# Zero rows of the later experts written inside the experts' loop of a one-core mixture-of-experts kernel

## The chip, the cores and the metric

The kernel runs on one core of a Trainium2 chip. The metric is the device time of one execution in microseconds (us); of several runs the median is taken. A core has five engines that work side by side, each through its own instructions in their order: TensorE (PE, matmuls and transposes), VectorE (DVE), ScalarE (ACT), GpSimd (POOL) and SyncE (SP). In this kernel SP does nothing but issue transfers (DMAs); ACT issues a few, and POOL issues all those whose rows are chosen by an index. Engines wait for each other and for transfers through semaphores.

## The reference, cut to what matters

The input `x` is 8,192 tokens of 256 numbers. It is normalised; one branch runs a gated recurrence over it, the other a mixture of 32 experts, of which each token takes four, plus a shared expert. The two are multiplied and added to `x`.

```python
xn = _layernorm(x)
s = recurrence(xn, W_in, b_in, W_g, b_g, W_out, b_out)
# ffn(xn):
w, idx = _gate(xf, wg)                      # 4 of 32 experts a token
cap = int(1.25 * N * K / E)                 # 1280 slots an expert
pos = (jnp.cumsum(oh, axis=0) * oh).sum(-1) - 1
dest = jnp.where(pos < cap, fe * cap + pos, E * cap)
xe = xp[buf_tok].reshape(E, cap, DIM)       # slots without a token are zero
h = silu(xe @ w1) * (xe @ w3)
out = (h @ w2) * buf_w
y = zeros.at[buf_tok].add(out)              # back to the tokens
z = (silu(xf @ sw1) * (xf @ sw3)) @ sw2     # shared expert
return x + s * silu(y + z)
```

So an expert has up to 1,280 slots, filled from the front with the tokens that chose it. How many are filled is known only when all tokens have been routed.

## The kernel before, in words

**First stage.** The tokens come in nine batches (`RTS`, 512, 512, then 1,024 each). For each batch the kernel normalises, turns rows into columns on PE, computes gates and logits, chooses experts on DVE (`choose`), finds each token's slot (`place`), and scatters the token's row into a DRAM buffer `xd_d` by POOL (`dispatch`, `send`, L517 to L527): one indirect DMA for 128 tokens and one of their four choices. A row is `XR` = 289 floats (1,156 bytes): the 256 features, 32 weights, and the token's number. The batches of the last round are sent by column of choice, the fourth first, since the slots are sorted downward: rows of expert 0 can stand only in the fourth column, rows of expert 1 in the third or fourth, and so on. Beside that the shared expert is computed for 16 chunks of 512 tokens; its output `zt` of a chunk is stored to `y_d` by a DMA (`shared_out`, L573 to L582) that SP issues, for the last two chunks ACT.

**Zero rows.** `xd_d` gives each expert 1,280 rows and 128 more. When all batches are routed, `ends()` (L535) computes on DVE, for each expert, the row behind its last token (`last[0, 1, e]`), and for each tile of 128 slots where to read it (`start`). `fill(e0, e1)` (L529 to L533) then has SP write, for each expert from `e0` to `e1`, 128 rows of zeros (`hole`) from that row on: a value load of the row number into a register, then a DMA of 144.5 KB. It is called four times, each time for a quarter of the experts: the first quarter right behind `ends()`, the second behind the output of shared chunk 12, both in the batch loop's turn r = 8 (L717 and L724), the third and the fourth in the turn r = 9 (L696 and L724), which has no batch of its own, only the rest of the shared expert and of the recurrence. In this turn SP first loads expert 0's weights (L690).

**Experts' loop.** `load_slots(e, i)` (L746 to L760) has SP read expert e's slots: part i of `spans`, 512, 512 and 256 slots, so 4, 4 and 2 DMAs of 128 rows, each behind a value load (L753, L754). Tiles `xe` of parts 0 and 1 share four buffers, those of part 2 two. Tile's tracking of `xd_d` makes each read wait for what wrote to it; the calls of `declare_no_dep` and `add_manual_dep` there replace that, for the first experts, by waits for the columns that can hold their rows. `load_expert(e)` (L117) loads 3 x 256 KB of weights into one of two buffers. Ahead of the loop SP has: the three parts of expert 0, the weights of expert 1, the three parts of expert 1 (L954 to L958).

A turn of the loop (L964) for expert e: SP issues parts 0 and 1 of expert e + 2; `hidden(e)` computes both projections, in sums and differences of quarter blocks so that seven products do the work of eight; PE then turns expert e + 1's slots (`turn`, L795); `first_out(e)` and `rest(e)` do the second projection and POOL adds the weighted rows to `y_d` at their tokens (L871); SP loads the weights and part 2 of expert e + 2.

All engines except POOL run in the order in which the code is written (`manual_schedule`). Within the first expert this order is, on DVE: `weight_sums(0)`, the blocks `B` of `second_blocks` (L809 to L812), `targets(0)` (`rf`, L769, which reads the last column of all three parts), then the sums `u`, `v` of `hidden(0)` (L826). On ACT: the copies into `B` (L803, L804, L808), `weights(0)` (`wt`, L776, which reads all three parts), then `p` (L841) and the copies of `v` (L846). On PE: `turn(0, 0)`, `turn(0, 1)`, four first products (`put`, L820), three added ones (`add_to`, L823), the same again for the second projection:

```python
            put(0, w(0, 0), B[:, 0])
            nc.scalar.copy(p, ps[0])
            put(1, S[:, 1, i], B[:, 4])
            plus(u, p, ps[1])
```

**Semaphores of transfers.** The transfers that SP and ACT issue take eight completion semaphores in turn, in the order of the program. An issue waits until the transfer before it on the same semaphore has landed.

**Tail.** 16 chunks of `y_d` are read back, passed through silu, multiplied by the recurrence's output and added to `x`.

Of the kernel before, what the change touches and what calls it, by code (L numbers as in the profile page):

```python
# [8 lines left out]
F32 = mybir.dt.float32  # L9
# [7 lines left out]
def recurrent_moe_kernel(  # L17
# [18 lines left out]
    nc = tc.nc  # L36
    P = 128
# [3 lines left out]
    E = wg.shape[0]  # L41
    H = w1.shape[2]
    K = 4
# [13 lines left out]
    XR = D + E + 1  # L57
# [4 lines left out]
    NR = len(RTS)  # L62
# [5 lines left out]
    FIRST = P  # L68
    END = FIRST + E * EP
# [10 lines left out]
    keep = ctx.enter_context(tc.tile_pool(name="keep", bufs=1))  # L80
# [8 lines left out]
    xd_d = dram.tile([END + P, XR], F32, name="xd_d")  # L89
# [6 lines left out]
    last = keep.tile([1, 2, E], I32, name="last")  # L96
# [7 lines left out]
    def apart(key, ins):  # L104

        tc.declare_no_dep(ins.ins, group=key, reason="different rows")
        tc.add_to_no_dep_group(key, ins.ins)
# [9 lines left out]
    def load_expert(e):  # L117
        w = wpool.tile([P, 3, KD, H], F32, tag="w", name=f"w_{e}")
        for i, src in enumerate((w1, w3, w2)):
            nc.sync.dma_start(out=w[:, i], in_=src[e].rearrange("(k p) h -> p k h", p=P))  # L120
        return w
# [20 lines left out]

    ET = mybir.EngineType
    engines = {ET.PE, ET.DVE, ET.Activation, ET.SP}
    with tc.tile_pool(name="ab", bufs=1) as ab, tc.tile_pool(name="xp", bufs=4) as xp, tc.tile_pool(
        name="rt", bufs=2
    ) as rt, tc.tile_pool(name="sh", bufs=2) as sh, tc.manual_schedule(engines=engines):
# [2 lines left out]
        def load_x(r):  # L150
            xt = xp.tile([P, RT, XR], F32, tag="xt", name=f"xt_{r}")
            for h in range(0, RTS[r], CT):
                nc.sync.dma_start(out=xt[:, h : h + CT, 0:D], in_=batch(x_f, r)[:, h : h + CT, :])
            xts[r] = xt
# [15 lines left out]
        for i, src in enumerate((sw1, sw3, sw2)):  # L170
# [8 lines left out]
            out=tri, in_=tri, compare_op=ALU.is_gt, fill=0.0, base=0, pattern=[[1, P]], channel_multiplier=-1  # L179
# [4 lines left out]
        for r0, n in ((0, 2), (2, NR - 2)):  # L184
            q = RTS[r0]
# [19 lines left out]
        hole = ab.tile([P, XR], F32, name="hole")  # L205
# [27 lines left out]
        with nc.allow_non_contiguous_dma(reason="a bias, once"):  # L233
# [13 lines left out]
            out=y_d[N : N + CAP, :].rearrange("(i p) d -> p i d", p=P),  # L247
            in_=hole[:, 0:D].unsqueeze(1).to_broadcast([P, EJ, D]),
# [278 lines left out]
                tc.add_to_no_dep_group(f"column{column}", ins.ins)  # L527

        def fill(e0, e1):  # L529

            for e in range(e0, e1):
                row0 = nc.sync.value_load(last[0:1, 1, e : e + 1], min_val=FIRST, max_val=END - P)  # L532
                apart("xd", nc.sync.dma_start(out=xd_d[bass.ds(row0, P), :], in_=hole))  # L533

        def ends():  # L535

# [147 lines left out]
        for r in range(4, NR + 1):  # L684
            new = r < NR
            c = 2 * (r - 2)
            if r + 2 < NR:
                load_x(r + 2)
            if r == NR:
                first_w = load_expert(0)  # L690
            if new:
                to_features(r, 0)
            project(r - 1, 0)
            shared_out(c - 1, late)
            if r == NR:
                fill(2 * E // 4, 3 * E // 4)  # L696
            if new:
                l0 = features(r, 0)
                to_features(r, 1)
            project(r - 1, 2)  # L700
            if new:
                l1 = features(r, 1)
                lg = ps_tp.tile([P, RT, E], F32, tag="tp", name=f"lg_{r}")
                logits(lg, l0, 0)
                logits(lg, l1, 1)
                M, cum, ex = choose(r, lg)
                weigh(r, M, ex)
            hT = shared_hidden(c)
            project(r - 1, 4)
            project(r - 1, 6)  # L710
            if new:
                pc = count(r, cum)
                put = place(r, M, cum, pc)
                dispatch(r, put)
                if r + 1 == NR:
                    ends()
                    fill(0, E // 4)  # L717
                recur(unit[r])
            if r + 1 < NR:
                norm(r + 1)  # L720
            shared_out(c, hT)
            if r + 1 >= NR:
                q = 2 * (r + 1 - NR) + 1
                fill(q * E // 4, (q + 1) * E // 4)  # L724
            late = shared_hidden(c + 1)
            if new:
                order_states(r)
            if r + 2 < NR:
                scale(r + 2)
# [8 lines left out]
    with tc.tile_pool(name="fin", bufs=NX, reuse_waits="tile") as fin, tc.manual_schedule(  # L738
        engines=engines
    ), ExitStack() as stack:  # L740
        mp = stack.enter_context(tc.tile_pool(name="moe", bufs=2, reuse_waits="tile"))
        ws, xes, rows, wts, Ss, Bs, hTs = {0: first_w}, {}, {}, {}, {}, {}, {}

        rows_of = mybir.DependencyInfo(mybir.DependencyClass.Sync, mybir.DependencyReason.DATA)

        def load_slots(e, i):  # L746
            s0, n = spans[i]
            xe = xes[e, i] = mp.tile(
                [P, n // P, XR], F32, tag=f"xe{n}", bufs=4 if n == CW else 2, name=f"xe_{e}_{s0}"
            )  # L750
            for j in range(n // P):
                q = s0 // P + j
                row0 = nc.sync.value_load(start[0:1, e, q : q + 1], min_val=FIRST - P, max_val=END - P)  # L753
                ins = nc.sync.dma_start(out=xe[:, j, :], in_=xd_d[bass.ds(row0, P), :])  # L754
                for k in range(K - 1 - e):
                    tc.declare_no_dep(ins.ins, group=f"column{k}", reason="no rows of this expert")
                if e < K - 1 and j == 0:
                    for k, name in sent:
                        if k is None or k >= K - 1 - e:
                            tc.add_manual_dep(ins.ins, name, rows_of, reason="rows of this expert")  # L760
# [53 lines left out]
        def hidden(e):  # L814

            B, S = Bs.pop(e), Ss.pop(e)
            h = hTs[e] = mp.tile([P, KH, 2, CW], F32, tag="h", bufs=1, name=f"h_{e}")

            def put(n, a, b):
                nc.tensor.matmul(ps[n], a, b, start=True, stop=True)  # L820

            def add_to(n, a, b):
                nc.tensor.matmul(ps[n], a, b, start=False, stop=True, skip_group_check=True)  # L823

            def plus(to, a, b):
                nc.vector.tensor_tensor(to, a, b, ALU.add)  # L826

            def gate(m, t, src):

                if i == 0:  # L830
                    nc.scalar.activation(h[:, m, t], src, AF.Silu)
                else:
                    nc.vector.tensor_tensor(h[:, m, t], h[:, m, t], src, ALU.mult)  # L833

            for i in range(2):
                w = lambda k, m: ws[e][:, i, k, m * P : (m + 1) * P]
                ps = [ps_mm.tile([P, CW], F32, tag="mm", name=f"ps{n}_{e}_{i}") for n in range(4)]
                p, u, v = (mp.tile([P, CW], F32, tag=n, bufs=1, name=f"{n}_{e}_{i}") for n in "puv")
                c = h[:, 1, 1] if i == 0 else mp.tile([P, CW], F32, tag="c", bufs=1, name=f"c_{e}")
# [4 lines that stand above are left out]
                put(2, S[:, 0, i], B[:, 3])  # L844
                plus(v, u, ps[2])
                nc.scalar.copy(ps[2], v)  # L846
                put(3, S[:, 2, i], B[:, 5])
                plus(c, v, ps[3])
                plus(ps[3], u, ps[3])
                add_to(0, w(1, 0), B[:, 1])  # L850
                gate(0, 0, ps[0])
                gate(1, 1, c)
                add_to(2, S[:, 3, i], B[:, 2])
                add_to(3, w(1, 1), B[:, 6])
                gate(1, 0, ps[3])
                gate(0, 1, ps[2])
# [94 lines left out]
            xr[c] = pool.tile([P, CT, D], F32, tag="xr", name=f"xr_{c}")  # L951
            nc.sync.dma_start(out=xr[c], in_=chunk(x_f, c))

        for i in range(3):  # L954
            load_slots(0, i)
        ws[1] = load_expert(1)
        for i in range(3):
            load_slots(1, i)  # L958
        weight_sums(0)
        first_blocks(0, *turn(0, 0))  # L960
        second_blocks(0, *turn(0, 1))
# [2 lines left out]
        for e in range(E):  # L964
            new = e + 1 < E
            if e + 2 < E:
                load_slots(e + 2, 0)
                load_slots(e + 2, 1)
            hidden(e)
            if new:  # L970
                first_blocks(e + 1, *turn(e + 1, 0))
                weights(e + 1)
                weight_sums(e + 1)
                targets(e + 1)
            first_out(e)
            if new:
                second_blocks(e + 1, *turn(e + 1, 1))
            rest(e)
            if e + 2 < E:
                ws[e + 2] = load_expert(e + 2)  # L980
                load_slots(e + 2, 2)
            if e % 2 == 1 and e // 2 < NX:
                load_residual(e // 2, fin)
# [53 lines left out]
```

## Time and profile before

| | us |
|---|---|
| median of 3 runs | 1161.77 (1160.72 to 1162.23) |
| profiled execution | 1353.81 |
| its span, first to last instruction | 1352.1 |

| engine | busy us | share | instructions |
|---|---|---|---|
| PE | 1079.8 | 80% | 3882 |
| PE weight loads | 665.1 | 49% | 3882 |
| DVE | 695.6 | 51% | 1899 |
| ACT | 504.2 | 37% | 976 |
| POOL | 684.8 | 51% | 552 |

The profiled execution is 192 us longer than the runs. Of the span, some 564 us are the first stage, 737 the experts and 51 the tail. A row of the profile's timeline gives start, length, engine, line, operation, the tiles written and read, and in brackets the idle time before it and what ended it. "SPq" and "ACTq" rows are issues of transfers; their length is that of the issue, not of the transfer. TensorE's granted clock stands as a share of full speed.

| transfers in the profile | count | KB each |
|---|---|---|
| slot loads, xe from xd_d (SP) | 320 | 144.5 |
| weights of experts (SP) | 96 | 256 |
| zero rows, xd_d from hole (SP) | 33 | 144.5 |
| zt to y_d (SP / ACT) | 14 / 2 | 512 |
| rows of tokens to xd_d (POOL) | 256 | |
| outputs added to y_d (POOL) | 274 | |

### The profile page before, as it was taken

The numbers are of one execution on the slowest core, as the hardware profiler recorded it, in microseconds if no ns is written. First come the engines' busy times: TensorE is split into PE (matmuls) and PEld (weight loads), VectorE is DVE, ScalarE is ACT, GpSimd is POOL, SyncE is SP. The second block draws the span as 40 slices with busy tenths as digits, with TensorE's granted clock in tenths as the row PEclk, the third lists the DMA queues.
The fourth block names the chain that finished last, engine by engine and source line by source line (L and its number), as shares of the span: only waits on it lengthen the run. The fifth ranks groups of instructions, "written<-read, shape, count | busy, mean of one in ns | idle before, by whom it ended". The sixth has DMA issues, their size and how long they took to land.

```text
span 1352.1 us, 15840 instructions
## 1 busy us (share of the span) xinstructions
PE 1079.8 (80%) x3882; PEld 665.1 (49%) x3882; DVE 695.6 (51%) x1899; ACT 504.2 (37%) x976; POOL 684.8 (51%) x552
## 2 busy tenths in 40 slices
PE   5771929575757485699999999999999999999930
PEld 2351516343434253356656565656565656656520
DVE  7750835352526060156555565655565565656538
ACT  1430504232323130144444444444444444444432
POOL 3655260727172727034655646565655556565540
PEclk9885969787778787799999999999999999999975
DMA  6332231414131315477686778786878787887678
GB/s 188 123 134 107 78 109 38 163 53 156 40 132 47 132 64 183 160 178 156 120 190 143 165 152 175 163 172 145 185 155 180 138 200 167 171 179 144 116 179 357
DMA packets 149834, 197.26 MB, mean 146 GB/s; under 512 B 17705, under 2 KB 133330, under 8 KB 149714
## 3 DMA queue, kind: packets, MB, share of 16 engines
q0 software_dynamic: 51744, 73.83, 29.0%
q1 hardware_dynamic: 97074, 120.70, 28.6%
q10 hardware_dynamic: 896, 1.36, 0.3%
q8 instruction: 48, 0.79, 0.3%
q14 instruction: 72, 0.59, 0.1%
HBM read 99.05 MB, written 96.76 MB: 145 GB/s over the span
## 4 chain that ended last, share of the span: by engine, by line
PE 53%; DVE 3%; SPq 2%; issue 1%; DMA 1%; POOL 0%; ACT 0%; POOLq 0%; DVEq 0%; ACTq 0%
PE eo L866 17%; PE ps L820 16%; PE ps L823 12%; PE ep L795 4%; PE xu L102 2%; DVE y L996 1%; DVE xr L997 1%; SPq L532 1%; SPq L533 0%; DMA y<-y_d 0%; POOL y_d L871 0%; DMA y_d<-ob,row 0%; SPq L753 0%; PE xh L921 0%; PE xp L904 0%
## 5 line engine op out<-in xcount | busy, mean ns | idle before, releaser
L871 POOL DMA_INDIRECT y_d<-ob,row x274 | 422.4, 1542 | 342.9 <-DVE rf L769 262.0
L518 POOL DMA_INDIRECT xd_d<-xt,put x256 | 255.3, 997 | 275.2 <-DVE put L512 108.3
L866 PE MATMUL eo<-w,h 128*128 128x256 f32 x1024 | 237.1, 379 | 0.4 <-DVE h L833 0.4
L866 PEld LDWEIGHTS eo<-w,h 128*128 128x128 f32 x1024 | 188.5, 190 | 31.3 <-issue 8.8
L820 PE MATMUL ps<-B,S 128*128 128x512 f32 x384 | 176.4, 595 | 0.3 <-DVE B L811 0.3
L868 ACT ACTIVATE ob<-eo,wt 128x256 f32<-128x256 f32 x274 | 118.8, 471 | 130.7 <-PE eo L866 127.1
L826 DVE TENSOR_TENSOR u<-p,ps 128x512 f32<-128x512 f32 x64 | 44.0, 688 | 185.5 <-PE ps L820 182.4
L823 PE MATMUL ps<-B,w 128*128 128x512 f32 x256 | 130.8, 592 | 0.0
L820 PEld LDWEIGHTS ps<-B,S 128*128 128x128 f32 x384 | 73.3, 191 | 93.8 <-issue 77.6
L102 PE MATMUL pz<-sw,hT_s 128*128 128x256 f32 x256 | 64.1, 404 | 29.9 <-ACT s_all L409 25.2
L102 PE MATMUL po<-Wio,xnT 128*128 128x256 f32 x256 | 70.0, 396 | 16.6 <-issue 11.2
L846 ACT COPY ps<-v 128x512 f32<-128x512 f32 x64 | 37.7, 590 | 120.4 <-DVE v L826 97.5
L102 PE MATMUL pf<-xnT,Wf 128*72 128x512 f32 (+1 forms) x72 | 48.4, 801 | 41.1 <-issue 36.7
L409 ACT COPY s_all<-po 128x512 f32<-128x512 f32 x32 | 18.7, 585 | 162.7 <-remote 94.4
L795 PE MATMUL ep<-ident,xe 128*128 128x128 f32 x512 | 69.6, 278 | 11.2 <-DMA xe<-xd_d 11.2
L823 PEld LDWEIGHTS ps<-B,w 128*128 128x128 f32 x256 | 48.0, 189 | 62.2 <-issue 31.1
L795 PEld LDWEIGHTS ep<-ident,xe 128*128 128x128 f32 x512 | 61.0, 143 | 33.0 <-DMA xe<-xd_d 23.5
L340 DVE COPY xnT<-xp 128x512 f32<-128x512 f32 x13 | 8.9, 688 | 127.8 <-remote 80.7
L102 PEld LDWEIGHTS pz<-sw,hT_s 128*128 128x128 f32 x256 | 50.8, 203 | 40.0 <-ACT s_all L409 25.6
L102 PE MATMUL pa_s<-xnT,sw 128*128 128x512 f32 x128 | 68.6, 663 | 0.4 <-ACT Gt L365 0.4
L820 PE MATMUL ps<-B,w 128*128 128x512 f32 x128 | 66.3, 600 | 0.0
L823 PE MATMUL ps<-B,S 128*128 128x512 f32 x128 | 66.2, 599 | 0.1
(168 smaller groups left out, 1504.7 us busy)
## 6 DMA issues: line engine op xcount, KB each, us to landing
xe<-xd_d SPq DMA_DIRECT2D x320, 144.5 KB
w<-in_L_ffn_w_dram SPq DMA_DIRECT2D x96, 256.0 KB
xt<-in_L_attn_x_dram SPq DMA_DIRECT2D x16, 512.0 KB
xr<-in_L_attn_x_dram SPq DMA_DIRECT2D x16, 512.0 KB
y<-y_d SPq DMA_DIRECT2D x16, 512.0 KB
out_dram<-xr SPq DMA_DIRECT2D x16, 512.0 KB
y_d<-zt SPq DMA_DIRECT2D x14, 512.0 KB
xd_d<-hole SPq DMA_DIRECT2D x33, 144.5 KB
```

Source lines behind the costliest of these rows:

```text
L102: nc.tensor.matmul(ps, lhsT, rhs, start=(i == 0), stop=(i == len(pairs) - 1))
L409: nc.scalar.copy(s_all[:, at_j : at_j + 2, :], po)
L518: ins = nc.gpsimd.indirect_dma_start(out=xd_d, out_offset=bass.IndirectOffsetOnAxis(ap=index, axis=0), in_=rows, in_offset=None,)
L532: row0 = nc.sync.value_load(last[0:1, 1, e : e + 1], min_val=FIRST, max_val=END - P)
L795: nc.tensor.transpose(ps[:, j * P : (j + 1) * P], xes[e, i][:, j, k * P : (k + 1) * P], ident)
L820: nc.tensor.matmul(ps[n], a, b, start=True, stop=True)
L823: nc.tensor.matmul(ps[n], a, b, start=False, stop=True, skip_group_check=True)
L826: nc.vector.tensor_tensor(to, a, b, ALU.add)
L846: nc.scalar.copy(ps[2], v)
L866: nc.tensor.matmul(po[:, i, :], hT(m), ws[e][:, 2, m, :], start=(m == 0), stop=(m == KH - 1))
L868: nc.scalar.activation(ob[:, q % 2, :], po[:, i, :], AF.Copy, scale=wts[e][:, q : q + 1])
L871: nc.gpsimd.indirect_dma_start(out=y_d, out_offset=bass.IndirectOffsetOnAxis(ap=rows[e][:, q : q + 1], axis=0), in_=ob[:, q % 2, :], in_of ...
```

## The change

The zero rows of experts 0 to 15 are still written in the first stage, where the first two quarters were. Those of experts 16 to 31 are no longer written there: turn e of the experts' loop, for e from 0 to 15, writes those of expert 16 + e, behind the loads of parts 0 and 1 of expert e + 2 and ahead of `hidden(e)`. They come from a second tile of zeros, `hole_m`, which is allocated in the loop's pool and set by DVE ahead of `weight_sums(0)`. Each slot load is freed from the tracked waits for all zero rows, and the first load of each part is given a wait for its own expert's alone; the writes in the loop likewise don't wait for the loads of other experts. The waits for the columns of the last batch now cover expert 3 too. And the order ahead of the loop is changed: parts 0 and 1 of expert 0, the weights of expert 1, parts 0 and 1 of expert 1, then part 2 of expert 0 and part 2 of expert 1.

```diff
+    filled = {}
+
+    def fill_expert(e, hole):
+
+        row0 = nc.sync.value_load(last[0:1, 1, e : e + 1], min_val=FIRST, max_val=END - P)
+        ins = nc.sync.dma_start(out=xd_d[bass.ds(row0, P), :], in_=hole)
+        apart("xd", ins)
+        tc.declare_no_dep(ins.ins, group="loads", reason="other experts' rows")
+        tc.add_to_no_dep_group("fills", ins.ins)
+        filled[e] = ins.ins
+
...
         def fill(e0, e1):
-
             for e in range(e0, e1):
-                row0 = nc.sync.value_load(last[0:1, 1, e : e + 1], min_val=FIRST, max_val=END - P)
-                apart("xd", nc.sync.dma_start(out=xd_d[bass.ds(row0, P), :], in_=hole))
+                fill_expert(e, hole)
...
             shared_out(c - 1, late)
-            if r == NR:
-                fill(2 * E // 4, 3 * E // 4)
...
             shared_out(c, hT)
-            if r + 1 >= NR:
-                q = 2 * (r + 1 - NR) + 1
-                fill(q * E // 4, (q + 1) * E // 4)
+            if r + 1 == NR:
+                fill(E // 4, E // 2)
...
+        hole = mp.tile([P, XR], F32, tag="hole", bufs=1, name="hole_m")
+        nc.vector.memset(hole, 0.0)
...
                 ins = nc.sync.dma_start(out=xe[:, j, :], in_=xd_d[bass.ds(row0, P), :])
+                tc.add_to_no_dep_group("loads", ins.ins)
+                tc.declare_no_dep(ins.ins, group="fills", keep=[filled[e]], reason="other experts' rows")
...
-                if e < K - 1 and j == 0:
+                if j == 0:
+                    tc.add_manual_dep(ins.ins, filled[e].name, rows_of, reason="rows of this expert")
+                if e < K and j == 0:
...
-        for i in range(3):
-            load_slots(0, i)
-        ws[1] = load_expert(1)
-        for i in range(3):
-            load_slots(1, i)
+        for e in range(2):
+            for i in range(2):
+                load_slots(e, i)
+            if e == 0:
+                ws[1] = load_expert(1)
+        for e in range(2):
+            load_slots(e, 2)
...
                 load_slots(e + 2, 1)
+            if e < E // 2:
+                fill_expert(E // 2 + e, hole)
             hidden(e)
```

## The prediction

> **What bounds the kernel.** I read first the busy time by stage, cut where the experts' loop begins and where the tail begins; columns are stretch, length, busy time of PE, weight loads, DVE, ACT and POOL, granted clock, DMA share, GB/s.
>
> ```profile
> 0.00:564.00 564.00, 355.77 (x1234) 219.98 (x1234) 242.95 (x1035) 155.30 (x206) 262.38 (x278) 0.81 0.32 112
> 564.00:581.00 17.00, 9.26 (x21) 4.63 (x22) 3.31 (x10) 2.83 (x7) 0.00 (x0) 0.50 0.51 147
> 581.00:1301.00 720.00, 714.72 (x2628) 440.45 (x2626) 411.46 (x823) 329.18 (x747) 420.14 (x273) 1.00 0.77 159
> ```
>
> From 581 to 1301 us the TensorE has work without a gap: 720/32 = 22.5 us an expert at full clock. Nothing off PE can shorten that. The change aims at the 17 us ahead of it, where PE is busy 9 and its clock is halved. So next I read that seam, on SP's queue and then on PE.
>
> ```profile
> 508.65 30.37 SPq L533 DMA_DIRECT2D xd_d<-hole  x8
> 539.73 2.79 SPq L120 DMA_DIRECT2D w<-in_L_ffn_w_dram  x3
> 542.54 0.00 SPq L582 DMA_DIRECT2D y_d<-zt  x1
> 543.60 18.46 SPq L533 DMA_DIRECT2D xd_d<-hole  x16
> 564.87 10.92 SPq L754 DMA_DIRECT2D xe<-xd_d  x10
> 575.84 1.46 SPq L120 DMA_DIRECT2D w<-in_L_ffn_w_dram  x3
> ```
>
> Sixteen zero-row writes stand directly ahead of the first slot load: 21.3 us, 543.60 to 564.87. PE's last matmul of the shared part ends at 560.2 (call it E), and its next one waits:
>
> ```profile
> 567.07 0.47 PE L795 MATMUL ep<-ident,xe 128*128 128x128 f32 x1 [6.87 <-DMA xe<-xd_d]
> 576.52 1.92 PE L820 MATMUL ps<-B,w 128*128 128x512 f32 x2
> ```
>
> What opens the first expert fully is DVE's first `u` (L826); from there PE runs on. It needs `p` from ACT, which in its turn stands behind `wt` of the last two slot tiles (L776), as `rf` (L769) does on DVE:
>
> ```profile
> 560.85 0.34 ACTq L582 DMA_DIRECT2D y_d<-zt  x1
> 577.78 0.19 ACT L776 COPY wt<-xe 128x2 f32<-128x2 f32 x1 [0.96 <-DMA xe<-xd_d]
> 578.48 0.58 ACT L841 COPY p<-ps 128x512 f32<-128x512 f32 x1 [0.50 <-PE ps L820]
> 580.96 0.69 DVE L826 TENSOR_TENSOR u<-p,ps 128x512 f32<-128x512 f32 x1 [0.74 <-PE ps L820]
> ```
>
> So before: u = 580.96 = E + 20.8.
>
> **The sixteen writes taken out ahead of the loads.** They free 21.3 us of SP, so the first loads could issue near 543.6. Were this all, PE would go on at E: transposes 1.0, copies 1.2, transposes 1.0, then `B` on ACT and DVE and put(1), about 6 to 7 us to u: a gain of some 14 us in this profile. But two things in the built order of instructions and their waits stand against it.
>
> **First, the wait on zt_15.** SP's and ACT's transfers take eight completion semaphores in turn, and each issue waits for the landing of the one eight issues before. With the sixteen writes gone, the eight slot loads of expert 0 follow directly on zt_13, zt_14 and zt_15 in that round, and the eighth load waits for zt_15 itself. ACT issues zt_15 at 560.85, after PE's last shared matmul; its semaphore steps land at 563.69 to 563.94. So the eighth load, and all that SP has behind it, starts at Z = 563.9 = E + 3.7, only 1 us ahead of the old *first* load. Queued behind it on SP are expert 1's weights, its slots, and expert 0's last two slot tiles. Before, the same wait was met, but the queue came to it at 573.1, when it was long over.
>
> **Second, the moved slot tiles.** The last two slots of expert 0 (span 2) were SP's 9th and 10th load; now they stand behind w_1 (3 transfers) and expert 1's eight loads. `wt` (ACT) and `rf` (DVE) still stand ahead of p and u, and both engines go in order. From rows of before: eighth load Z + 0.1; to w_1's first issue 0.4; from there to expert 1's first load 2.5 (575.84 to 578.34); seven more 7.9 (578.34 to 586.24); expert 0's two 1.25 + 1.13; landing 2.25 (issued 575.46, landed 577.71); then wt, p and u's start 1.1 as before. Sum 16.6: u = 563.9 + 16.6 = 580.5, against 580.96. A gain of 0.4 us in this profile, where the edit alone looked like 14.
>
> **The clock.** In the new order PE does the transposes and puts by about 572 and then waits some 8 us for p. The row above (6.87 us idle) was followed by a granted clock of 0.5 until 580.89, and the puts at 576.5 took 1.06 us instead of 0.59. The Trainium skill ("TensorE: Matmul & The Clock Gate", Part 1) says that an idle window of about 3.4 us halves the clock, and about 3.4 us of sustained work restores it: a rule against this change. Before, the cold stretch is over when u starts. Afterwards PE restarts cold at p: from u to the end of add_to(3) before 4.1 us; now add_to(2) can't start before v's copy (u + 2.2), then two cold pairs of 1.7 against 0.86: some 5.3. By the rows +1.2 us; by the rule up to half a window, 1.7, or of two, 3.4. I take 1.2, since the rows show the work there. In this profile: -0.4 + 1.2 = +0.8, a span near 1352.9.
>
> **The sixteen writes moved into the loop.** Each adds on SP a value load and a transfer, 1.13 us, and 148 KB. SP has room:
>
> ```profile
> SPq L120 <- PE eo L866: 245.0, 30, 13.6
> ```
>
> That is 8.2 us an expert in which SP waits for PE before it loads the weights. PE hides all; without this cover it would be 16 x 1.13 = 18 us. The write for expert 16 + e stands fourteen turns ahead of its reader. DMA: 148 KB per 22.5 us is 6.6 GB/s on 159, share 0.77 to about 0.80. Bounds 0 and 18 us; 0 taken. The new memset (1,156 bytes a partition, DVE) lies in the 18.5 us that DVE waits there: 0. Expert 3's first load now names all the scatters, which ended on POOL at 538: 0.
>
> **From the profile to the runs.** The profiled execution took 1353.81 us (span 1352.1 and 1.7 around it), the runs 1161.77: 192 us less. The loop has no room for that, so it is the first stage, which shows it: between 508 and 543 eight writes and three weight loads took SP 34 us, and PE stood still 20 us, while POOL kept its pace. I take these stalls to be the profiler's. At the paces elsewhere (1.2 us a write, 0.5 a weight load, matmuls at full clock) SP would be 22.8 us earlier there and PE 20.1. So in the runs the first slot load of before lies at E + 4.7 - 2.7 = E + 2.0, and u at E + 18.1; after the change u hangs on zt_15 alone, E + 20.3. Difference +2.2, the clock +1.2: **+3.4 us, 1165.2 us**.
>
> Let d be the distance from E to the old first load in the runs. The change costs 20.3 - (16.1 + d) + 1.2 = 5.4 - d. All hangs on d, which no row shows: 4.7 in the profile; least -5, where the old order too is held by zt_15 (its u then E + 11.5, so +10 us); most about 10.
>
> **Rivals.**
> A (forecast), d from 0 to 4: +1.4 to +5.4, 1163 to 1167. Chance 0.47.
> B, faster or level: without the profiler's stalls the third set of writes runs beside the last scatters (POOL sends until 41 us after its first at 496.8) and the two share the DMA engines, so before loses more than I count. The skill ("DMA: Bandwidth & Descriptors", Issuing engines are not separate DMA queues) says that transfers of all issuers interleave on the same 16 engines. Rows: writes alone 0.35 share at 120 GB/s (545 to 550), writes and scatters 0.63 at 217 (498 to 508). Together they fit, so no rate is lost by the rows; if they got in each other's way by 0.4 us a write, d grows by 6. It turns faster from d = 5.4. At d = 10, 1157.2. Chance 0.27.
> C, slower still: SP is quicker in the runs, d below 0: 1167 to 1171.8. For it: [...] against: the paces outside the stalls are steady. Chance 0.17.
> D, the change does what it looks like: the wait on zt_15 does not bind because it lands early, and span 2 lands in time: u at E + 7 instead of E + 18.1, -11: 1150.7. Against it: issue and landing rows of zt_15. Chance 0.05.
> E, the loop's writes are not hidden: +18, 1180. Against it: SP's wait row. Chance 0.04.
>
> **The numbers.** About 0.2% (2.3 us) is what a measurement can tell from no change. Faster: B beyond d = 7.7 and D, 0.20. Same: the low part of A (0.15) and of B (0.12), 0.27. Slower: 0.32 of A, C and E, 0.53. Range: B's end to C's end, 1157 to 1171.5; D and E are left out. A's own range is 1163 to 1167.
>
> **What would show it.** The eighth load of expert 0 issued right after zt_15's landing, with six loads far ahead; 14 us later the last two slots of expert 0; PE idle some 8 us between its first puts and add_to(0) and a clock of 0.5 after it; the loop at 22.5 us an expert. Wrong: the eighth load issued before 563, or u before E + 17, or PE gaps in the first sixteen experts.

## The result, and the profile after

| | us |
|---|---|
| before, median of 8 runs | 1162.00 (1160.32 to 1163.84) |
| after, median of 8 runs | 1158.63 (1155.98 to 1160.68) |
| ratio, 95% interval | 0.9972 [0.9959, 0.9985] |
| profiled execution of after, its span | 1157.49, 1155.8 |

The changed kernel is faster by 0.28%, 3.3 us. The forecast was 1165.2, slower by 3.4 us: the time lies inside the range, the sign is wrong. One thing must be known to read the numbers: on one of the chips used below (B) every run of every kernel takes some 200 us longer, all of it in the first stage, and so did the profiled execution of before, but neither its timed runs nor the profile of after.

The busy time of after by stage (stretch, length, busy time of PE, weight loads, DVE, ACT and POOL, granted clock, DMA share, GB/s), cut at the last shared matmul and at the first `u`:

```profile
0.00:362.50 362.50, 328.67 (x1236) 211.05 (x1237) 243.31 (x1036) 154.71 (x205) 259.31 (x270) 0.97 0.49 166
362.50:383.00 20.50, 8.05 (x25) 3.86 (x23) 3.33 (x9) 3.22 (x8) 7.69 (x8) 0.78 0.69 216
383.00:1101.00 718.00, 715.21 (x2624) 440.17 (x2624) 411.54 (x823) 329.52 (x748) 418.03 (x271) 1.00 0.77 161
```

The loop is as full as before, 715 of 718 us. The first stage is 200 us shorter than in the profile of before, and the seam between the two is still there, 20.5 us long with PE busy for 8. POOL, idle in the seam before, now works in it: its scatters have not ended. SP's queue at the seam, then SP's own waits in the whole execution (us in total, times, longest):

```profile
341.70 0.41 SPq L591 DMA_DIRECT2D y_d<-zt  x1
346.86 20.16 SPq L762 DMA_DIRECT2D xe<-xd_d  x8
367.06 1.50 SPq L120 DMA_DIRECT2D w<-in_L_ffn_w_dram  x3
369.61 2.63 SPq L762 DMA_DIRECT2D xe<-xd_d  x3
```

```profile
SPq L120 <- PE eo L878: 232.6, 30, 12.0
...
SPq L762 <- DMA y_d<-zt: 10.6, 2, 9.0
```

The sixteen writes are gone from between `zt` and the slot loads, and the first load goes out 15.7 us ahead of E, the end of the last shared matmul (362.54). But the eighth of the eight loads, which would take 9 us back to back, ends only at 367.02: it waited 9.0 us for `y_d<-zt`, as the prediction said. The engines behind it (PE, ACT and DVE, each from its own timeline, and the stage's row for the stretch from the first `u` on, with the granted clock third from the end):

```profile
369.30 1.33 PE L807 MATMUL ep<-ident,xe 128*128 128x128 f32 x5 [4.53 <-DMA xe<-xd_d]
383.15 2.08 PE L835 MATMUL ps<-B,w 128*128 128x512 f32 x2 [6.92 <-ACT p L853]
```

```profile
363.20 0.34 ACTq L591 DMA_DIRECT2D y_d<-zt  x1
382.14 0.19 ACT L788 COPY wt<-xe 128x2 f32<-128x2 f32 x1 [11.43 <-DMA xe<-xd_d]
382.51 0.59 ACT L853 COPY p<-ps 128x512 f32<-128x512 f32 x1 [0.18 <-DVE row L782]
```

```profile
383.13 0.69 DVE L838 TENSOR_TENSOR u<-p,ps 128x512 f32<-128x512 f32 x1 [0.62 <-ACT p L853]
```

```profile
383.15:387.15 4.00, 3.94 (x4) 1.34 (x5) 2.65 (x4) 1.71 (x3) 0.00 (x0) 0.50 0.45 113
```

ACT's `wt` waits 11.43 us for the moved part 2 of expert 0; `p` and `u` stand behind it; PE idles 6.92 us and then, at a granted clock of 0.50, takes 2.08 us for two matmuls that take 1.02 at full clock. The first `u` is at E + 20.6; 20.3 was forecast. So the kernel after behaves as predicted, and the error has to be looked for in the kernel before.

### The profile page after: what moved, and what is told of

Its sections match the earlier page's. It is cut to its first block, busy times and chain, and to the rows that moved or that the text cites. A ratio compares the mean times of both kernels' runs of the same rounds, so it can differ in the third digit from the quotient of the medians.

```text
span 1155.8 us, 15845 instructions
## 1 busy us (share of the span) xinstructions
PE 1051.9 (91%) x3882; PEld 655.1 (57%) x3882; DVE 696.0 (60%) x1900; ACT 504.4 (44%) x976; POOL 689.7 (60%) x552
## 4 chain that ended last, share of the span: by engine, by line
PE 77%; DVE 10%; ACT 3%; POOL 3%; issue 3%; DMA 2%; SPq 1%; POOLq 0%; DVEq 0%; ACTq 0%
PE eo L878 20%; PE ps L832 19%; PE ps L835 14%; PE ep L807 5%; PE po L102 4%; PE pb_s L102 3%; PE pa_s L102 3%; POOL xd_d L529 3%; PE xu L102 3%; PE pf L102 2%; DVE y L1012 2%; PE pz L102 2%; DVE st L313 1%; DVE xr L1013 1%; ACT Gt L376 1%
## 5 line engine op out<-in xcount | busy, mean ns | idle before, releaser
L529 POOL DMA_INDIRECT xd_d<-xt,put x256 | 260.0, 1015 | 104.8 <-issue 75.0
L807 PE MATMUL ep<-ident,xe 128*128 128x128 f32 x512 | 67.2, 274 | 5.3 <-DMA xe<-xd_d 4.5
L843 ACT ACTIVATE h<-ps 128x512 f32<-128x512 f32 x96 | 53.8, 595 | 31.9 <-PE ps L835 31.9
L102 PE MATMUL po<-Wio,xnT 128*128 128x256 f32 x256 | 65.8, 380 | 0.2 <-DVE bo L305 0.2
L102 PE MATMUL pb_s<-xnT,sw 128*128 128x512 f32 x128 | 61.9, 607 | 3.2 <-ACT Gt L376 3.2
L845 DVE TENSOR_TENSOR h<-h,ps 128x512 f32<-128x512 f32 x96 | 62.8, 682 | 3.2 <-PE ps L835 0.2
L102 PE MATMUL pa_s<-xnT,sw 128*128 128x512 f32 x128 | 63.0, 615 | 0.0
L102 PE MATMUL pz<-sw,hT_s 128*128 128x256 f32 x256 | 59.2, 383 | 1.1 <-ACT zt L590 0.7
L821 DVE TENSOR_TENSOR B<-ep,B 128x512 f32<-128x512 f32 x32 | 22.1, 692 | 56.6 <-PE ep L807 27.3
```

Source lines behind the costliest of these rows:

```text
L102: nc.tensor.matmul(ps, lhsT, rhs, start=(i == 0), stop=(i == len(pairs) - 1))
L529: ins = nc.gpsimd.indirect_dma_start(out=xd_d, out_offset=bass.IndirectOffsetOnAxis(ap=index, axis=0), in_=rows, in_offset=None,)
L807: nc.tensor.transpose(ps[:, j * P : (j + 1) * P], xes[e, i][:, j, k * P : (k + 1) * P], ident)
```

## The experiments

Four chips, on each the kernel before timed beside the runs: A (the runs e1 to e4), B (e5, e7, e8, e9), C (e10 to e13, later e18) and D (e14 to e17). For all traces I use the same marks: E; the first slot load; the first `u`; the second `u`; the end. The rows are collected in a table behind the runs.

### e1: the kernel before, a second trace

No edit.

> The kernel before, profiled once more, to see its seam without the stalls that its first profile had in the first stage (its span was 192 us over the runs). Theory 1 (the third set of sixteen writes collides with the last scatters): the scatters run some 10 us beyond PE's last shared matmul E, the DMA engines are full (share 0.95 or more) during the third set, the writes take 1.5 us or more each instead of 1.13, and the first slot load issues at E + 7 to E + 10, u at E + 24 to E + 26. Rival (SP's pace alone, as in the prediction): writes at 1.13 to 1.2 us each, first slot load at E + 2, u at E + 18; then the 3 us gained came from somewhere else, from a first stage that ended earlier or from a faster loop.

Measured: 1160.2 us, a span of 1158.5, without the stalls of the first profile. POOL's scatters don't end 23 us ahead of E as there but 10 us behind it, the first slot load is at E + 5.0, not E + 2.0, and the first `u` at E + 20.9. From E to the end it takes 791.9 us, where the changed kernel's trace takes 793.2. Theory 1 has the overlap right and its price too high: the sixteen writes take 20.2 us, 1.26 each and not 1.5, and load and `u` come earlier than it says. Of the rival's figures the load and `u` are missed too. This one pair explains no gain; the later traces do.

### e2, e3, e4: one counterweight of the change taken away, then both

The changed kernel with the old order of the slot parts (e2), with the stores of zt_14 and zt_15 issued by POOL instead of ACT, so that no slot load comes to wait for them (e3), and with both (e4).

```diff
-        for e in range(2):
-            for i in range(2):
-                load_slots(e, i)
-            if e == 0:
-                ws[1] = load_expert(1)
-        for e in range(2):
-            load_slots(e, 2)
+        for i in range(3):
+            load_slots(0, i)
+        ws[1] = load_expert(1)
+        for i in range(3):
+            load_slots(1, i)
```

```diff
-            (nc.scalar if c + 3 > NC else nc.sync).dma_start(out=chunk(y_d, c), in_=zt)
+            (nc.gpsimd if c + 3 > NC else nc.sync).dma_start(out=chunk(y_d, c), in_=zt)
```

> The changed kernel with expert 0's last two slot tiles put back to SP's 9th and 10th load, ahead of expert 1's weights and slots. Theory (the moved tiles hold up wt and rf, so p and u): the two land at about 372 on the changed kernel's time axis instead of 382; u moves from 383.1 to about 376, where p next waits for the last scatters to land (375), and PE's 7 us gap ahead of add_to(0) shrinks to 2 or less: about 1150.5 us, ratio to before 0.990. Rival (only zt_15 and the scatters count, the moved tiles don't): no more than 1 us from the changed kernel, 1158.

> The changed kernel with the stores of shared chunks 14 and 15 issued by POOL instead of ACT, so that they no longer stand in the round of eight semaphores that SP's slot loads go through. Theory (the wait of the eighth load on zt_15 blocks SP's queue for 10 us): expert 0's eight loads are all out by 357, its last two land by 372, and u comes at about 376, held by the scatters through p: about 1150.5 us. Rival (the queue is held by something else, the scatters or the DMA engines): SP's loads come at the same times as now and the time stays at 1158.

> Both edits at once: old order of expert 0's slot tiles, and chunks 14 and 15 stored by POOL. If p's wait for the last scatters is what is late next, it gains little over either alone: u at 376, about 1150 us. If the scatters don't hold p, u comes at about 369 and the time is about 1144 us.

Measured against before at 1159.66 (12 runs): e2 1153.86, ratio 0.9953 [0.9933, 0.9973]; e3 1152.82, 0.9940 [0.9919, 0.9961]; e4 1153.08, 0.9942 [0.9921, 0.9963]. First `u` at E + 15.2, 13.7 and 14.4. The changed kernel was not timed in this set; in its own trace the first `u` is at E + 20.6. So either edit alone brings 5 to 7 us and both together no more: something third stands right behind. All three times lie 2 to 3 us over the 1150 expected; the first `u` lies up to 1.7 us behind the expected one, which is E + 13.5 on the axis of after's trace. The copy `p` on ACT in e4's timeline names it:

```profile
367.25 0.39 ACT L788 COPY wt<-xe 128x4 f32<-128x4 f32 x3
378.56 0.58 ACT L853 COPY p<-ps 128x512 f32<-128x512 f32 x1 [10.92 <-DMA xd_d<-xt,put]
```

`wt` is done at 367.6, PE has `ps0` at 368, and `p` waits until 378.56 for scatters of the first stage. The buffer of `p` shares bytes with `put`, the scatters' index tile, so it would have to wait for the last scatter to land; e7 and e16 put this to the test.

### e5: the moved slot parts, alone on the kernel before

The edit is the first diff above the other way round, on the kernel before.

> The kernel before with one edit: the slot tiles of part 2 of experts 0 and 1 are loaded after parts 0 and 1 of both, as the change has it; all zero rows stay where they were. Theory (SP's order sets the start of expert 0): part 2 of expert 0 goes out behind 8 more tiles (9.4 us) and lands about 11 us later than now, ACT's `wt` and DVE's `rf` wait for it, and both stand ahead of `p` and `u`; the first `u` goes from 19.9 us after the last shared matmul to about 30, and the time from about 1160 to 1170. Rival (part 2 is hidden anyway, since expert 0's blocks are what is late): no change, 1160.

Measured on chip B: 1367.75 against 1357.83, ratio 1.0077 [1.0043, 1.0111], so 10.5 us slower. The first slot load stays at E + 2.7; the first `u` goes to E + 27.3, against E + 18.2 in e9 on the same chip, and a colder clock adds 1.0 us up to the second `u`. ACT's timeline shows what holds it:

```profile
588.69 0.19 ACT L776 COPY wt<-xe 128x2 f32<-128x2 f32 x1 [11.60 <-DMA xe<-xd_d]
```

The theory holds: the reordering alone costs 10 us, and in the change the earlier start of the loads has to make up for that.

### e7, e16: the third holder taken away as well

e4 with `c` allocated ahead of `p`, which moves `p` off the bytes of `put`:

```diff
             h = hTs[e] = mp.tile([P, KH, 2, CW], F32, tag="h", bufs=1, name=f"h_{e}")
+            late = mp.tile([P, CW], F32, tag="c", bufs=1, name=f"c_{e}")
...
-                c = h[:, 1, 1] if i == 0 else mp.tile([P, CW], F32, tag="c", bufs=1, name=f"c_{e}")
+                c = h[:, 1, 1] if i == 0 else late
```

> The run e4 (old slot order, last two stores of the shared expert's output by POOL) with the one tile `c` allocated ahead of `p`, so that `c` and not `p` shares bytes with the scatters' index tiles `put`. Theory (the last scatters' landing holds `p`): ACT's copy `p` goes out when PE has `ps0`, about 3 us after the first slot blocks, the first `u` comes about 5 us after the last shared matmul instead of 14.4, and the time is 9 us under e4: about 1144. Rival (something else of that moment, the landing of part 2 or the DMA engines' load, is right behind): u about 11 us after the last shared matmul, 1150; if the shared bytes don't matter at all, 1153.

> The run e7 again (old slot order, last two stores of the shared expert's output by POOL, `c` and not `p` on the bytes of `put`). On a chip where the kernel before takes some 1160 us, theory (the landing of the last scatters held `p`): first `u` 5 to 9 us behind the last shared matmul, time about 1144, ratio 0.987. Rival (the DMA engines' load holds the slot loads up by as much): 1150 or more, ratio 0.992 or more.

Measured: e7 on chip B 1342.10 against 1357.83, ratio 0.9885 [0.9832, 0.9937]; e16 on chip D 1145.06 against 1163.19, ratio 0.9842 [0.9822, 0.9862]. The absolute time expected of e7 did not take chip B into account; e16 has it, 1145 for 1144. This version beats both kernels. SP, ACT and DVE of e16, from their timelines (its profiled execution took 1139.81, the shortest of its five, through an earlier E):

```profile
346.52 11.29 SPq L762 DMA_DIRECT2D xe<-xd_d  x10
```

```profile
364.31 0.59 ACT L854 COPY p<-ps 128x512 f32<-128x512 f32 x1 [0.35 <-PE ps L833]
```

```profile
366.81 0.69 DVE L839 TENSOR_TENSOR u<-p,ps 128x512 f32<-128x512 f32 x1
```

All ten loads of expert 0 are out before E (361.10), `p` waits for PE alone, and the first `u` is at E + 5.7, in e7's trace too. This is the "gain of some 14 us" that the edit looked like, by the ratios some 16 us on B and 18 on D; three waits hid it: zt_15, the moved part 2, and the last scatter behind `p`.

### e8, e11, e14: the changed kernel timed again; e9, e10, e15: more traces of the kernel before

No edits.

> The changed kernel once more, for a second trace and its time beside the kernel before on one chip. Theory L (the gain is made after the last shared matmul: the kernel before mostly starts its slot loads later than the 5.0 us after it that the one look showed): ratio 0.997, first `u` again about 20.6 us after the last shared matmul. Rival F (the two kernels are equal from the last shared matmul on, and the 3.4 us are a draw of the first 90 us of the program, which vary by 4 us from execution to execution): ratio within 0.999 and 1.001 over these runs.

> The kernel before once more, for a third trace. Theory L: the first slot load 8 to 9 us after the last shared matmul, first `u` 23 to 24 us after it. Rival F: 5 us and 20 us again.

> The kernel before once more, for its trace. Theory (place of the first slot load): where POOL's last 32 scatters overlap the sixteen writes, that is where they end behind the last shared matmul, the first slot load of before stands 5 us or more behind that matmul and the change gains; where they end 20 us ahead of it, it stands 2 us behind it and the change loses 2 to 4 us. So this look shows one of the two pairs: scatters' end at plus 11 and load at plus 5 or more, or scatters' end at minus 23 and load at plus 2. Rival (the load's place has nothing to do with POOL): a pair that crosses them.

> The changed kernel once more, timed. Theory: faster by about 3 us if the kernel before takes some 1160 us on this chip (scatters overlap the third set), slower by 2 to 5 us if it takes some 1355 (they don't). Rival: the same sign either way.

> The changed kernel once more, timed in five rounds. Theory N (behind the last shared matmul the change costs about 1.4 us where the scatters overlap, as two pairs of traces show: first `u` 0.4 us earlier, then 1.25 us of halved clock and 0.6 us in the loop; a median that says faster comes from the first 90 us of the program, which vary by 4 us from execution to execution): ratio between 0.999 and 1.003. Rival G (there is a real gain of some 3 us that these traces don't catch): ratio 0.996 to 0.998. On a chip where the kernel before takes some 1355 us both expect 1.001 to 1.005.

> The kernel before once more, for its trace: theory N, from the last shared matmul to the end 792 us (789 where the scatters end before it), first slot load at plus 5 to 6. Rival G: 795 or more, first slot load at plus 8 or later.

Measured, after against before on the same chip: B 1362.17 against 1357.83, ratio 1.0029 [1.0009, 1.0048], slower; C 1159.25 against 1160.41, 0.9994 [0.9983, 1.0005], the same; D 1159.46 against 1163.19, 0.9963 [0.9950, 0.9976], faster. What was expected of e8 and e9 was missed by both theories, since both spoke of a chip without stalls; e11's theory was missed too (same, not faster). e10 showed the pair that its theory named, scatters beyond E and the load at E + 5.8. e14 and e15 went to rival G: the gain on D is real, and the kernel before is late there in its own trace. The end of POOL's scatters, SP's queue and SP's wait in e9 (B, E = 564.11), then in e10 (C, E = 363.74) and e15 (D, E = 363.91):

```profile
540.44 0.96 POOL L518 DMA_INDIRECT xd_d<-xt,put  x1 [0.30 <-issue]
```

```profile
546.27 18.06 SPq L533 DMA_DIRECT2D xd_d<-hole  x16
566.21 10.95 SPq L754 DMA_DIRECT2D xe<-xd_d  x10
```

```profile
SPq L754 <- DMA xd_d<-hole: 0.7, 1, 0.7
```

```profile
373.78 0.96 POOL L518 DMA_INDIRECT xd_d<-xt,put  x1 [0.30 <-issue]
```

```profile
343.98 20.17 SPq L533 DMA_DIRECT2D xd_d<-hole  x16
369.56 11.12 SPq L754 DMA_DIRECT2D xe<-xd_d  x10
```

```profile
SPq L754 <- DMA xd_d<-hole: 4.1, 1, 4.1
```

```profile
344.21 19.79 SPq L533 DMA_DIRECT2D xd_d<-hole  x16
375.22 10.93 SPq L754 DMA_DIRECT2D xe<-xd_d  x10
```

```profile
SPq L754 <- DMA xd_d<-hole: 9.9, 1, 9.9
```

SP needs nearly the same time for the sixteen writes, 18.1 us on B and some 20 elsewhere. What differs is the pause between the last write and the first load: 2 us on B, 11 on D, of which 9.9 are a wait for the landing of a zero-row write. In e10 this wait is 4.1 us, in e1 3.2. The stretches of the writes, of the wait and of what follows, in e15, then the stretch of the writes in e9:

```profile
344.00:364.00 20.00, 19.49 (x73) 13.41 (x71) 3.49 (x7) 4.18 (x8) 15.12 (x17) 1.00 1.07 282
364.00:375.20 11.20, 0.00 (x0) 0.00 (x0) 0.00 (x0) 0.54 (x1) 8.40 (x9) 0.72 0.83 245
375.20:390.00 14.80, 8.00 (x20) 4.13 (x21) 2.83 (x6) 2.83 (x7) 0.00 (x0) 0.52 0.58 161
```

```profile
546.00:564.20 18.20, 17.69 (x50) 10.96 (x50) 4.05 (x8) 4.60 (x9) 0.00 (x0) 0.84 0.47 172
```

With POOL at work beside them (15.12 us of 20, against 0) the DMA share is 1.07 instead of 0.47: the DMA engines are full, and a backlog is left when SP has issued the last write. From issue to landing a write of the first two quarters takes 2.9 us in e10 (median of sixteen), one of the last two 6.3; in e15 it is 3.1 and 8.3. On B the scatters have ended, but B differs in other ways too; no run takes them away on one of the other chips.

The marks of the traces, those of the first three columns relative to E (the chip of the first profiles is not known):

| trace | chip | last scatter issued | first slot load | first u | first to second u | second u to end | E to end |
|---|---|---|---|---|---|---|---|
| before, first profile | | -22.9 | +4.7 | +20.8 | 6.07 | 765.1 | 791.9 |
| before, e9 | B | -23.7 | +2.1 | +18.2 | 6.23 | 764.7 | 789.1 |
| before, e1 | A | +10.0 | +5.0 | +20.9 | 5.95 | 765.1 | 791.9 |
| before, e10 | C | +10.1 | +5.8 | +21.2 | 5.95 | 764.9 | 792.1 |
| before, e15 | D | +10.0 | +11.3 | +26.5 | 5.99 | 765.1 | 797.6 |
| after | | +9.0 | -15.7 | +20.6 | 7.18 | 765.5 | 793.2 |
| after, e8 | B | -22.7 | -16.6 | +19.5 | 7.20 | 764.8 | 791.5 |
| after, e11 | C | +10.3 | -13.2 | +20.6 | 7.24 | 765.8 | 793.6 |
| after, e14 | D | +8.7 | -15.5 | +20.4 | 7.50 | 764.6 | 792.5 |

The kernel before moves with the landing of its last zero rows, first `u` from E + 18.2 to E + 26.5. The kernel after hardly moves, 19.5 to 20.6. What a trace shows ahead of E varies too: E lies between 361.1 and 366.5 in the traces without stalls, whatever the kernel, and the spread is there after the first 90 us. So a total of one execution says little here, and the marks behind E say much.

### e12, e13: SP's time and the writes' bytes apart

e7 with sixteen more writes at the old place, into a DRAM buffer that nobody reads: of 16 columns (e12), of all 289 (e13).

```diff
+        def fill_spare(e0, e1):
+            for e in range(e0, e1):
+                row0 = nc.sync.value_load(last[0:1, 1, e : e + 1], min_val=FIRST, max_val=END - P)
+                apart("spare", nc.sync.dma_start(out=spare[bass.ds(row0, P), 0:16], in_=hole[:, 0:16]))
...
+            if r == NR:
+                fill_spare(2 * E // 4, 3 * E // 4)
```

> The run e7 with sixteen more transfers on SP where the kernel before had the third and fourth quarter of the zero rows, each with its value load, into a spare DRAM buffer that nobody reads, but of 16 columns of the row's 289 only: SP's time without the bytes. Theory: SP reaches the first slot load about 20 us later than in e7, just at the last shared matmul, and the first `u` comes about 15 us after that matmul instead of 9 or less: 6 to 10 us over e7. Rival (SP has slack there): as e7.

> As the run with 16 columns, with all 289 columns: SP's time and 2.3 MB of writes. Where POOL's scatters run beside them, theory (they get in each other's way on the DMA engines): 2 to 5 us over the narrow run, SP's value loads and issues slower than 1.1 us a pair and the slot loads landing later. Rival (they fit side by side, as the prediction took it): within 1 us of the narrow run. Where the scatters have ended before: within 1 us by both.

Measured on chip C: e12 1154.81, ratio 0.9951 [0.9934, 0.9967]; e13 1155.91, 0.9962 [0.9949, 0.9975]. Some 10 us over e16's 1145 (another chip), about the upper end of the 6 to 10 expected for SP's time; the first `u` comes at E + 18.7 in e12, not 15. The bytes add 1.1 us between the two medians, less than the intervals are wide, less than theory and near the rival, although the DMA engines are full with them. The stretch of the writes in e12, then in e13:

```profile
344.30:364.20 19.90, 19.32 (x73) 13.35 (x71) 3.74 (x8) 4.25 (x8) 15.02 (x17) 1.00 0.62 189
```

```profile
345.60:365.60 20.00, 19.25 (x73) 13.28 (x71) 3.74 (x8) 4.42 (x8) 15.12 (x17) 1.00 1.05 284
```

Share 0.62 against 1.05 at the same pace of SP and POOL, and in both the first slot load goes out at E + 1.6. Here no load waits for all the spare writes to land. So full DMA engines did not slow the issuers; in e10 and e15 they cost the load that waits for the landing.

### e17: the loop's writes twice

```diff
                 fill_expert(E // 2 + e, hole)
+                row0 = nc.sync.value_load(last[0:1, 1, E // 2 + e : E // 2 + e + 1], min_val=FIRST, max_val=END - P)
+                apart("spare", nc.sync.dma_start(out=spare[bass.ds(row0, P), :], in_=hole))
```

> The changed kernel with each of the loop's sixteen zero writes issued a second time, with its value load, into a spare DRAM buffer. Theory (SP's wait for PE hides them, 8 us an expert): from the second `u` of expert 0 to the end 765.6 us as in the changed kernel, time as the changed kernel's. Rival (the 0.6 us by which this stretch is longer than in the kernel before are the writes'): 766.2. Rival E of the prediction (they are not hidden): plus 18 us.

Measured on chip D: 1158.91, against 1159.46 for the changed kernel; second `u` to end 765.0. Doubled writes cost nothing. SP's wait for PE in its trace:

```profile
SPq L121 <- PE eo L879: 214.4, 30, 10.9
```

In the four traces of the changed kernel it is 230.9 to 234.8 us, here 214.4: the sixteen writes more fill SP's idle time, as the prediction took it.

### e18: the narrowed wait, alone on the kernel before

All zero rows at their old place, old slot order, but a slot load waits for the zero rows of its own expert only (the change's wider wait for the last batch's columns, which also covers expert 3, is kept):

```diff
+                tc.add_to_no_dep_group("loads", ins.ins)
+                tc.declare_no_dep(ins.ins, group="fills", keep=[filled[e]], reason="other experts' rows")
...
+                if j == 0:
+                    tc.add_manual_dep(ins.ins, filled[e].name, rows_of, reason="rows of this expert")
```

> The kernel before with the narrowed waits alone: all four quarters of the zero rows at their old place, the old slot order, but each slot load waits for the zero rows of its own expert instead of all. Theory (what makes the kernel before late is that its first slot load waits for the landing of the last zero rows, written beside the last scatters): where the kernel before takes some 1160 us, first slot load 1.6 us behind the last shared matmul, first `u` 18.7 to 20 (landings of the writes still come back through the round of eight completion semaphores), from that matmul to the end 789 to 791 us; 2 to 7 us under the kernel before, with no move of the writes at all. Rival (the writes' bytes beside the scatters are the cost, whoever waits for them): as the kernel before. Where it takes some 1355, no difference by both.

Measured on chip C, in a later set: 1158.84 against 1162.87, ratio 0.9968 [0.9952, 0.9984], 3.7 us faster. That is about what the whole change gains against the kernel before at 1162 and 1163; the change itself was not timed in this set. The trace, SP's and PE's timeline, and the landing of the last zero-row write:

```profile
344.38 19.81 SPq L150 DMA_DIRECT2D xd_d<-hole  x16
367.49 12.07 SPq L763 DMA_DIRECT2D xe<-xd_d  x10
```

```profile
375.85 3.59 PE L808 MATMUL ep<-ident,xe 128*128 128x128 f32 x11 [11.81 <-DMA xe<-xd_d]
```

```profile
L150 SPq DMA_DIRECT2D xd_d<-hole x1: 332/332/332, 363.9 to 363.9; - x1
...
DMA to landing us min/median/max: 8.7/8.7/8.7
```

The gain is as expected, the way to it only in part. The first load is at E + 3.5 (E = 364.04), not 1.6: it still waits 2.1 us for one of the writes, through the round of completion semaphores. And it lands late: PE gets the first tile 8.4 us after its issue, against 3.8 in e10. First `u` E + 20.5, E to end 791.4, a little over the 789 to 791 expected and only some 0.6 under e10's. But e10 is another execution. In this one the last zero-row write landed at 372.6, E + 8.5; with its old wait the first load could not have gone out before that, if the write had landed at the same time. In the prediction's formula, 16.1 + d, a load at E + 8.5 puts the first `u` at E + 24.6, so by this estimate the narrowed wait saved some 4 us here, as much as the times say. The late tile is not the bytes alone: e13 has as many, and its first tile lands 3.8 us after its issue. In this trace as in e15 single completion steps come late.

## Why the prediction was wrong, by its own steps

- **The wait on zt_15, and the moved slot tiles: right.** Eighth load behind the landing of zt_15 (9.0 us of wait, row above), first `u` at E + 20.3 forecast, E + 19.5 to 20.6 in four traces. e3 takes the one away, e2 the other, and e5 shows the second alone at 10.5 us. That taking away either alone brings 5 to 7 us, and that `p` stands behind the last scatter too, the prediction did not say.
- **The clock: right.** +1.2 us forecast; from the first to the second `u` 7.18 to 7.50 in after, 5.95 to 6.23 in before. The granted clock was 0.50 there (row above). The estimate from the rule of the Trainium skill ("TensorE: Matmul & The Clock Gate", Part 1), 1.7 for one window of 3.4 us at half the clock, covers it too; the 3.4 of two windows did not come.
- **The sixteen writes in the loop: right.** 0 forecast; doubled they still cost 0 (e17).
- **The formula 5.4 - d: right in sign and order.** Its d is the first slot load of before, relative to E. By the traces of before it gives +3.3 on B (d = 2.1), -0.4 on C (5.8), -5.9 on D (11.3); measured +3.9 [+1.2, +6.5], -0.7 [-2.0, +0.6], -4.3 [-5.8, -2.8] us, so on D just outside. One trace a chip stands behind each d, and d changes from execution to execution. The pairs of traces, from E to the end, give +2.4, +1.5 and -5.1.
- **"From the profile to the runs", where d was taken as 2.0: the step that failed.** I took the stalls for the profiler's and moved SP and PE up by 22.8 and 20.1 us. I left out POOL. The stalls are not the profiler's: all 31 runs of before on B are some 200 us longer, and the profiles on A, C and D have none. Without the stalls POOL has no time to catch up. It sends 224 scatters almost in one go, from 77 to 374 us in e10, 1.3 us each as within the bursts of the first profile, and ends 10 us behind E instead of 23 ahead. So the third set of writes runs beside the last scatters, and the first slot load waits for them to land: d = 5.0, 5.8, 11.3, the last beyond the "most about 10". That d is 2.1 on B, and the change costs 3.9 us there as forecast, is luck: the 2.7 us taken off were for stalls that e9 still has.
- **Rival B named the place and the sign, with the wrong price.** I set it aside with "together they fit, so no rate is lost by the rows": 0.35 and 0.63 of share. For the writes of the first two quarters that holds: e10 has 0.62 at 220 GB/s from 322 to 332 us, and their landing takes 2.9 us. The last two quarters follow three weight loads and have two stores of `zt` beside them; there the share is 1.05 to 1.07. B's price was to be 0.4 us a write on SP; SP lost 0.1 (19.8 to 20.2 us against 18.1 for sixteen). The price fell on the landing of the last one. The 8-run result, -3.3 us, asks for a d of 8.7 by the formula; no trace of that set shows it, and the traces of before without stalls lie on both sides of it. That such a gain comes from this wait is shown by e18 and, in its trace, on D; for the set of the 8 runs it is inferred.

The Trainium skill ("DMA: Bandwidth & Descriptors", Queues, rings and completion order) says that a transfer's semaphore increment lands only after every earlier write from that DMA engine, across its queues. By this the zero rows' completion also waits for scatters queued ahead of it. The rows agree in direction, 0.7 us of wait without scatters and 3.2 to 9.9 with them; but beside scatters in engines that are not full a landing takes only 2.9 us (e10, above), where the last write of e9, without scatters, takes 2.0. So the order alone costs little here; how much of the rest is order and how much mere lack of bandwidth, no run here tells.

## What to carry to other kernels

When a profile is longer than the runs, do not only shorten the engines that stall in it: ask which engine the stalls had let catch up, because without them its backlog moves, and what it will then run beside. A queue of transfers that share DMA engines should be priced by who waits for the last landing, not by the issue rate; narrowing that wait (e18) gave here about as much as moving the work. And if an edit should bring 14 us and brings 3, look for each wait that ends next, in order: here a store's completion, a moved load, and two tiles that share bytes.

## What the runs showed of the hardware that was not expected

- **The same program takes 1160 us on one chip and 1358 on another.** On B, in the first stage, while POOL issues a run of scatters, the other engines come to a stop (in e9 PE and ACT for up to 27 us, DVE for up to 39) and go on about when the run ends. A stretch of e9 in which POOL alone works, and the copy on ACT with which it ends:

```profile
112.00:128.00 16.00, 0.00 (x0) 0.00 (x0) 0.00 (x0) 0.00 (x0) 12.04 (x14) 0.50 0.32 114
```

```profile
128.00 0.59 ACT L581 COPY zt<-pz 128x512 f32<-128x512 f32 x1 [16.25 <-remote]
```

PE had finished this `pz` at 105.7, and POOL's run of 32 scatters ends at 128.6. What ACT waited for the profile does not name ("remote"); the cause is open, and so is whether it is the chip or its condition at that time.
- **A late completion while the DMA engines are full.** The last zero-row write of e15 was issued at 363.66; fifteen of its sixteen completion steps came by 370.3, the last at 375.0. In e1 it took 4.7 us in all, in e18 8.7. Why one step of sixteen comes so late in some executions is open. The kernel before depends on it, and its median moved from 1159.7 to 1163.2 between sets, on chip C alone from 1160.4 to 1162.9, while the changed kernel's stayed within 1158.6 to 1159.5 (B left out).
